# First norm of the last four batches on x loaded with channels on partitions

## Chip, cores and metric

One core of a Trainium2 chip runs the whole program. The metric is the device time of one execution in microseconds (us), smaller is better. "About the same" means within 0.3% of the time before, which is about what a measurement of this kernel can tell from no change.

## The reference

One RWKV block in float32 on x of 8 batches, 256 tokens and 512 channels (32 heads of 16). Cut to what matters here:

```python
def _ln(x, w, b):
    m = jnp.mean(x, axis=-1, keepdims=True)
    v = jnp.mean((x - m) ** 2, axis=-1, keepdims=True)
    return (x - m) * jax.lax.rsqrt(v + EPS) * w + b
...
xn = _ln(x, ln1_w, ln1_b)                      # the first norm
sx = _token_shift(xn, state[:, i1])            # previous token minus this one
xxx = jnp.tanh((xn + sx * maa_x) @ maa_w1)...  # five mixes of xn and sx
w, r, k, v, g = ...                            # decay and four projections
s = k v^T + w * s;  out = r (u * k v^T + s)    # scan over 256 tokens, per head
x = x + groupnorm(out) * g @ Wo.T
xn2 = _ln(x, ln2_w, ln2_b)                     # the second norm
x = x + sigmoid(xr @ ffn_Wr.T) * (square(relu(xk @ ffn_Wk.T)) @ ffn_Wv.T)
```

The sums of a norm run over the 512 channels of one token; `w` and `b` are per channel.

## The kernel before

**Stages.** Each batch b goes through three functions: `inputs_of_scan` (line 677: first norm, mixes, projections of k, v, r, g and the decay w), `scan` (line 829: the recurrence over tokens) and `rest` (line 914: group norm, output projection, second norm, feed-forward). The stages of neighbouring batches overlap: while batch b is in its scan, batch b+1 or b+2 has its inputs made and batch b-1 its rest.

**Layouts.** Projections and the scan want channels on partitions and tokens along a row (tiles `xn`, `sx`, `mix`: 128 channels x 2 x 256 tokens, two of each per batch). x in DRAM has tokens first, so `load_x` (line 510) loads it with tokens on partitions, and `normed` (line 560) makes the norm there: for batches 2 to 7 ScalarE sums x and its squares (lines 571 and 575), takes the root as exp(-0.5 ln) (lines 556 and 558), and line 598 applies factor and shift, which in this layout are one number per partition, into `xh`. Then `turned` (line 603) turns `xh` with eight 128x128 transposes on TensorE per batch and norm (line 614, with the identity `idt`), ScalarE moves them out of PSUM with the channel's `ln_w` and `ln_b` (line 624), writes the first column (the previous row of the state, line 617), and GpSimd subtracts (line 628, tile `sx`).

**The scan.** A batch has 16 pieces of 128 partitions x 4 x 256. SyncE loads each piece of v from DRAM (tile `vs`, six buffers), ScalarE writes its first column (line 882), VectorE multiplies by k (line 889), VectorE scans (line 891), GpSimd multiplies by r (line 894), and after four pieces TensorE sums over the states (line 902).

**TensorE** does nearly all its matmuls through `mul` (line 430), either with all 128 columns of the array, or in four column tiles of 32, whichever the neighbours use. The trace writes them 128\*128 and 128\*32.

**The order of the work.** No scheduler at run time: `Plan` records every operation, and the table `TURNS` gives each its rank. `Plan.order` takes the operations by rank, as their inputs and buffers allow, and lays them into five fixed queues: TensorE, VectorE, ScalarE, GpSimd and SyncE (nearly all DMAs). Each queue runs strictly in its order, so an operation that waits holds back all behind it on that engine. Its tables `LATENCY`, `LANDS` and `TAKES` say how long it thinks that things take.

**Pools that matter.** `xt` (one buffer for the loaded x of batches 2 to 7), `xh` (2), `xn` (4), `x2` (2, x for the rest), `sq` (2, squares in the rest).

Of the kernel before, what the change touches and what calls it, by code (L numbers as in the profile page):

```python
# [12 lines left out]
P = 128  # L13
# [8 lines left out]
EPS = 1e-5  # L22
HALF = 0.5
# [47 lines left out]
class Plan:  # L71
# [5 lines left out]
    LANDS = {"vs__": (2.44, 1.6), "s": (0.1, 1.7), "vo_": (0.4, 1.9), "vo__": (0.46, 1.5), "o_": (0.4, 1.6), "x": (2.3, 1.1), "xt": (1.65, 2.1),  # L77
# [55 lines left out]
    def stage(self):  # L133
# [236 lines left out]
def tile_rwkv_block(  # L370
    ctx: ExitStack,
    tc: tile.TileContext,
    x: bass.AP,
    vecs: bass.AP,
    state: bass.AP,
    consts: bass.AP,
# [747 lines left out]
```

## Time and profile before

| what | value |
|---|---|
| median of 3 runs | 608.28 us (608.18 to 609.9) |
| the profiled execution's own time | 608.87 us |
| its span, first to last instruction | 607.1 us |
| TensorE busy | 597.6 us (98%) |
| VectorE busy | 531.2 us (87%) |
| ScalarE busy | 513.3 us (85%) |
| GpSimd busy | 505.4 us (83%) |
| granted TensorE clock | 1.0 |

In profile rows PE is TensorE, PEld its weight loads, DVE VectorE, ACT ScalarE, POOL GpSimd and SPq the queue of SyncE. "L614" is line 614 of the kernel before; the changed kernel has other numbers. A row of a group ends with busy us, mean ns of one instruction, then the idle time of the engine just ahead of them and what ended it. A row of the timeline begins with the start and the length in us. A float32 matmul is two instructions in the trace, a transpose is one. Ends of matmuls are modelled, so starts are used where a length matters.

### The profile page before, as it was taken

What the parts mean: (1) busy time and instruction counts of PE and PEld (TensorE: products, weight loads), DVE (VectorE), ACT (ScalarE), POOL (GpSimd) and SP (SyncE); (2) the same over time, 40 slices, a digit from 0 to 9 for tenths busy, and PEclk for the clock granted to TensorE, in tenths of its full rate; (3) what the DMA queues carried; (4) which work ended last, traced back from release to release, by engine and by line L of the source; (5) the groups of instructions that cost most, each with busy time, mean ns of one, the idle gap of its engine ahead of it and who ended that gap; (6) DMA issues with size and microseconds to landing.
All of it is one profiled execution on the core that took longest, in us unless ns stands there. A gap on an engine that the chain in (4) does not pass through costs nothing.

```text
span 607.1 us, 18838 instructions
## 1 busy us (share of the span) xinstructions
PE 597.6 (98%) x7892; PEld 344.4 (57%) x7892; DVE 531.2 (87%) x481; ACT 513.3 (85%) x1199; POOL 505.4 (83%) x385
## 2 busy tenths in 40 slices
PE   8999999999999999999999999999999999999997
PEld 7575655467444574377544774465644454745464
DVE  6699999899999989799798999999999999994332
ACT  4898879999999999999999999999998688963431
POOL 1699999999989897899979898989989989887030
PEclk9999999999999999999999999999999999999999
DMA  9796688898778868486589597795876798961551
GB/s 292 251 246 163 143 205 207 223 263 219 205 210 252 231 189 231 138 233 174 164 256 238 143 270 219 225 228 148 271 212 174 204 252 220 265 194 43 177 185 65
DMA packets 52500, 124.85 MB, mean 206 GB/s; under 512 B 5824, under 2 KB 11200, under 8 KB 52416
## 3 DMA queue, kind: packets, MB, share of 16 engines
q1 hardware_dynamic: 48048, 119.46, 71.8%
q10 hardware_dynamic: 4368, 4.20, 2.2%
q8 instruction: 62, 1.02, 0.7%
q14 instruction: 22, 0.18, 0.1%
HBM read 115.25 MB, written 8.39 MB: 204 GB/s over the span
## 4 chain that ended last, share of the span: by engine, by line
PE 88%; ACT 6%; DMA 4%; DVE 2%; issue 1%; SPq 0%; DVEq 0%; ACTq 0%
PE ps L430 73%; PE ps L902 9%; PE ps L614 2%; PE ps L766 2%; DMA Wk<-in_wk 2%; ACT ps L714 1%; DMA mw2a<-in_maa_w 1%; ACT sq L957 1%; DMA x<-in_x 1%; PE ps L928 1%; ACT L1048 1%; PE ps L844 1%; ACT rk L957 1%; ACT mix L984 0%; DVE x L974 0%
## 5 line engine op out<-in xcount | busy, mean ns | idle before, releaser
L891 DVE TENSOR_TENSOR_SCAN st<-wrep,vs 128x1024 f32<-128x1024 f32 x128 | 288.9, 2279 | 4.3 <-ACT wrep L872 2.2
L894 POOL TENSOR_TENSOR st<-st,r 128x1024 f32<-128x1024 f32 x128 | 254.2, 2002 | 11.3 <-DVE st L891 10.4
L889 DVE TENSOR_TENSOR vs<-vs,ps 128x1024 f32<-128x1024 f32 x122 | 144.6, 1208 | 9.3 <-ACT vs L882 6.5
L430 PE MATMUL ps<-Ws,mix 128*32 128x512 f32 (+2 forms) x804 | 114.7, 589 | 0.5 <-DVE x L974 0.2
L430 PEld LDWEIGHTS ps<-Ws,mix 128*32 128x32 f32 (+1 forms) x804 | 38.8, 118 | 62.7 <-issue 55.6
L726 POOL TENSOR_TENSOR mix<-mix,xn 128x512 f32<-128x512 f32 x62 | 67.0, 1096 | 7.7 <-DVE mix L720 6.8
L902 PE MATMUL ps<-st,con 128*32 128x256 f32 x1024 | 62.6, 380 | 0.3 <-DVE x L974 0.2
L430 PE MATMUL ps<-mix,Wg 128*32 128x256 f32 (+1 forms) x784 | 60.2, 379 | 0.3 <-ACT mix L983 0.2
L430 PE MATMUL ps<-mix,Wv 128*32 128x256 f32 (+1 forms) x832 | 59.9, 380 | 0.2 <-DVE mix L723 0.2
L430 PE MATMUL ps<-mix,Wr 128*32 128x256 f32 (+1 forms) x688 | 59.9, 380 | 0.0
L430 PE MATMUL ps<-mix,Wk 128*32 128x256 f32 (+1 forms) x880 | 59.4, 380 | 0.2 <-DMA Wk<-in_wk 0.2
L430 PE MATMUL ps<-mix,Ws 128*32 128x256 f32 (+1 forms) x784 | 58.2, 379 | 0.0
L430 PE MATMUL ps<-Ws,g 128*32 128x512 f32 (+1 forms) x416 | 57.1, 593 | 0.0
L1048 ACT ACT_TABLE_LOAD x39 | 50.0, 1283 | 1.1 <-ACT v L797 0.4
L647 POOL TENSOR_TENSOR mix<-mix,xn 128x512 f32<-128x512 f32 x44 | 47.2, 1093 | 3.1 <-ACT mix L645 2.9
L430 PEld LDWEIGHTS ps<-mix,Wr 128*32 128x32 f32 (+1 forms) x688 | 39.3, 123 | 17.9 <-issue 1.4
L714 ACT ACTIVATE ps<-ps,vec 128x256 f32<-128x256 f32 x112 | 45.7, 445 | 4.2 <-PE ps L430 2.7
L430 PEld LDWEIGHTS ps<-mix,Wv 128*32 128x32 f32 (+1 forms) x832 | 37.9, 116 | 19.5 <-issue 1.1
L902 PEld LDWEIGHTS ps<-st,con 128*32 128x32 f32 x1024 | 34.1, 110 | 26.3 <-issue 5.1
L430 PEld LDWEIGHTS ps<-mix,Ws 128*32 128x32 f32 (+1 forms) x784 | 39.6, 118 | 16.4 <-DVE mix L640 0.6
L430 PEld LDWEIGHTS ps<-mix,Wg 128*32 128x32 f32 (+1 forms) x784 | 38.4, 118 | 18.2 <-issue 1.0
L430 PEld LDWEIGHTS ps<-mix,Wk 128*32 128x32 f32 (+1 forms) x880 | 36.8, 114 | 20.6 <-issue 2.4
(116 smaller groups left out, 935.3 us busy)
## 6 DMA issues: line engine op xcount, KB each, us to landing
vs<-vo SPq DMA_DIRECT2D x128, 512.0 KB, 5.6
Ws<-in_wo SPq DMA_DIRECT2D x16, 512.0 KB, 6.6
Ws<-in_fr SPq DMA_DIRECT2D x16, 512.0 KB, 6.0
Ws<-in_fk SPq DMA_DIRECT2D x16, 512.0 KB, 5.6
Ws<-in_fv SPq DMA_DIRECT2D x16, 512.0 KB, 4.7
x<-in_x SPq DMA_DIRECT2D x9, 512.0 KB, 6.4
vo<-v ACTq DMA_DIRECT2D x15, 256.0 KB, 4.9
out<-o SPq DMA_DIRECT2D x15, 256.0 KB, 4.6
```

Of the source, the lines that this page charges most:

```text
L430: nc.tensor.matmul(out[i : i + n], lhsT=w[:, i : i + n], rhs=x, start=first, stop=final)
L614: nc.tensor.transpose(ps()[:, m, n * P : (n + 1) * P], xh[n]()[:, k * P : (k + 1) * P], idt())
L647: gp(512, t, [t, xn[q]], lambda q=q, t=t: nc.gpsimd.tensor_tensor(t(), t(), xn[q]()[:, :, 1 : T + 1], ALU.add))
L714: act(256, p_, [p_, vec], lambda g=g, q=q, m=m, p_=p_: nc.scalar.activation(p_()[:, m, :], p_()[:, m, :], AF.Identity, bias=col(f"maa_{g}" ...
L726: gp(512, t, [t, xn[q]], lambda q=q, t=t: nc.gpsimd.tensor_tensor(t(), t(), xn[q]()[:, :, 1 : T + 1], ALU.add))
L766: nc.tensor.matmul(pd()[i : i + 32, 0, :], lhsT=w, rhs=src[k // 2]()[:, k % 2, :], start=(k == begin), stop=(k == end))
L889: dve(4 * T, [vs], [vs, kp], lambda m=m, vs=vs, kp=kp: nc.vector.tensor_tensor(vs(), vs(), kp()[:, m : m + 1, :].to_broadcast([P, 4, T]), ...
L891: dve(4 * T, [st], [w, vs], lambda w=w, vs=vs, st=st: nc.vector.tensor_tensor_scan(st().rearrange("p n t -> p (n t)"), w().rearrange("p n ...
L894: gp(4 * T, st, [st, r], lambda m=m, st=st, r=r: nc.gpsimd.tensor_tensor(st(), st(), r()[:, m : m + 1, :].to_broadcast([P, 4, T]), ALU.mul ...
L902: nc.tensor.matmul(pat()[32 * i : 32 * i + 32, 0, :], lhsT=con()[:, s : s + 32], rhs=done[i]()[:, j, :], start=(j == 0), stop=(j == 3),)
L957: act(256, rsb, [rs], lambda blk=2 * q + n, n=n, rows=rows, rsb=rsb: nc.scalar.copy(by_block(rsb)[rows, n, :], rs()[32 * blk : 32 * blk + ...
L1048: nc.scalar.preload_act_table_set(TABLES[table])
```

## The change

For batches 4 to 7 the first norm no longer turns anything on TensorE. x is also given to the program as a second input `xt` with channels on partitions (made when the inputs are laid out, like the other layouts). The new function `ahead`:

- loads x with tokens on partitions, in two halves into `xh`, only for its sums, which are taken in place as before;
- puts factor and minus mean times factor side by side into a small tile `rn` (128 x 2 x 2), with the same ln and exp on ScalarE and the same small product on GpSimd;
- writes `rn` to DRAM (`ms`, 512 numbers of 4 bytes) and reads it back into a tile of the pool `sq` so that every partition holds all 256 factors and 256 shifts (`rb`, 256 KB written);
- loads `xt` into `xn`, multiplies by the factors on VectorE, adds the shifts on GpSimd, then applies `ln1_w` and `ln1_b` on ScalarE in place, and goes on as before.

Pool `xt` is gone, so batches 2 and 3 load x into `x2`; `xn` has six buffers. `LANDS` gets entries for the new loads. `TURNS` is new as a whole: the order changes from the first rows on, in batches 0 to 3 too.

```diff
+AHEAD = (4, 5, 6, 7)
...
     TURNS = """
-        11 45 15 38 49 98 95 96 109 46 94 72 220 97 55 62 64 140 16 14 26 20 27 43 18 54 58 17 40 48 19 60 61,
...
-    pool("xt", 1, [P, NT, E])
...
+    pool("rn", 1, [P, 2, NT])
-    pool("xn", 4, [P, 2, T + 1])
+    pool("xn", 6, [P, 2, T + 1])
...
+    pool("ms", 2, [2, T], dram)
...
     def load_x(b, kind):
-        if b or kind != "xt":
-            t = new("x2" if kind == "xt" and b == 1 else kind, f"{kind}{b}")
+        if kind != "xt" or b and b not in AHEAD:
+            t = new("x2", f"{kind}{b}")
             load(t, x[b].rearrange("(n p) e -> p n e", p=P), 524)
         else:
-            t = [new("sq", f"xt0_{n}") for n in range(NT)]
+            t = [new("xh" if b else "sq", f"xt{b}_{n}") for n in range(NT)]
...
+    def ahead(b):
...
+        act(2, rn, [mv, eh], lambda: nc.scalar.activation(
+            rn()[:, 0, :], mv()[:, :, 1], AF.Ln, bias=eh()[:, 0:1], scale=over), "exp", 1)
+        act(2, rn, [rn], lambda: nc.scalar.activation(rn()[:, 0, :], rn()[:, 0, :], AF.Exp, scale=-0.5), "exp")
+        gp(2, rn, [mn, rn], lambda: nc.gpsimd.tensor_tensor(rn()[:, 1, :], mn(), rn()[:, 0, :], ALU.mult), 30)
+        dma(ms, lambda: rn(), lambda: ms().rearrange("s (n p) -> p s n", p=P), 2, rn)
+        dma(rb, lambda: ms().rearrange("s t -> (s t)").unsqueeze(0).to_broadcast([P, 2 * T]),
+            rb, 262, ms)
...
+        for q in range(NQ):
...
+            dma(xn, lambda q=q: xt[b][:, 2 * q : 2 * q + 2, :], lambda xn=xn: xn()[:, :, 1 : T + 1], 262)
+            dve(512, [xn], [xn, rb], lambda xn=xn: nc.vector.tensor_tensor(
+                xn()[:, :, 1 : T + 1], xn()[:, :, 1 : T + 1], rb()[:, 0:T].unsqueeze(1).to_broadcast([P, 2, T]), ALU.mult))
+            gp(512, xn, [xn, rb], lambda xn=xn: nc.gpsimd.tensor_tensor(
+                xn()[:, :, 1 : T + 1], xn()[:, :, 1 : T + 1], rb()[:, T : 2 * T].unsqueeze(1).to_broadcast([P, 2, T]), ALU.add))
+            for m in range(2):
...
+                act(256, xn, [xn, vec], lambda m=m, k=k, xn=xn: nc.scalar.activation(
+                    xn()[:, m, 1 : T + 1], xn()[:, m, 1 : T + 1], AF.Identity, bias=col("ln1_b", k), scale=col("ln1_w", k)), pointers=2)
...
-        xn, sx = normed(load_x(b, "xt"), 1, 1, b, b == 0)
+        xn, sx = ahead(b) if b in AHEAD else normed(load_x(b, "xt"), 1, 1, b, b == 0)
...
+        "xt": x.reshape(NB, T, NK, P).transpose(0, 3, 2, 1),
```

Two places in the queues. On TensorE, between the projection of r in batch 4 (weights `Wr`) and that of g (`Wg`), the kernel before turns the first norm of batch 5 (`xh` is the norm with tokens on partitions; every row stands once more in the program, which is left out):

```order
L430 MATMUL ps_172<-mix_119,Wr_78 128x256 x2
L614 MATMUL ps_174<-idt,xh_86 128x128
L614 MATMUL ps_174<-idt,xh_87 128x128
...
L614 MATMUL ps_170<-idt,xh_86 128x128
L614 MATMUL ps_170<-idt,xh_87 128x128
...
L430 MATMUL ps_171<-mix_108,Wg_79 128x256 x2
L430 MATMUL ps_171<-mix_109,Wg_80 128x256 x2
```

In the changed kernel the same place on TensorE reads (line 435 is the old 430, 955 the old 902, the sum over states of the scan):

```order
L435 MATMUL ps_174<-mix_118,Wr_77 32x256 x8
L435 MATMUL ps_174<-mix_121,Wr_78 32x256 x8
...
L435 MATMUL ps_178<-mix_116,Wg_79 32x256 x8
L435 MATMUL ps_178<-mix_119,Wg_80 32x256 x8
L955 MATMUL ps_176<-st_161,con 32x256
L955 MATMUL ps_176<-st_156,con 32x256
```

The eight transposes are gone, and the projections around them, which ran with the full array (outputs of 128 partitions), now run in column tiles (32). Counted over the whole queue, TensorE changes between full array, column tiles and row tiles (the mixes and the decay) 82 times before and 72 times now, a transpose counted as full array; the transposes that are gone make no difference to the 82 by themselves.

On VectorE of the changed kernel, in the scan of batch 2, stand the two new products of batch 4 (line 715; 942 is the old 889, 944 the old scan 891, 961 the old 908, 802 the old 749):

```order
L942 TENSOR_TENSOR vs_149<-vs_149,ps_174 128x1024
L1027 TENSOR_TENSOR x_164<-ps_176,x_164 128x512
L961 TENSOR_TENSOR att_140<-ps_175,att_140 128x256
L961 TENSOR_TENSOR att_140<-ps_173,att_140 128x256
L944 SCALAR_TENSOR_TENSOR st_156<-wrep_172,vs_152 128x1024
L715 TENSOR_TENSOR xn_99<-xn_99,sq_163 128x2x256
L802 TENSOR_TENSOR mix_111<-ps_178,sx_107 128x256
L944 SCALAR_TENSOR_TENSOR st_157<-wrep_172,vs_149 128x1024
L715 TENSOR_TENSOR xn_101<-xn_101,sq_163 128x2x256
```

The same stretch of VectorE before (the scan of batch 2) has the scans and products without them:

```order
L974 TENSOR_TENSOR x_161<-ps_172,x_161 128x512
L908 TENSOR_TENSOR att_138<-ps_169,att_138 128x256
L891 SCALAR_TENSOR_TENSOR st_156<-wrep_168,vs_149 128x1024
L974 TENSOR_TENSOR x_161<-ps_173,x_161 128x512
L889 TENSOR_TENSOR vs_146<-vs_146,ps_170 128x1024
L749 TENSOR_TENSOR mix_106<-ps_171,sx_102 128x256
L749 TENSOR_TENSOR mix_108<-ps_169,sx_103 128x256
L891 SCALAR_TENSOR_TENSOR st_152<-wrep_168,vs_146 128x1024
```

Each new product is slipped in behind a scan; the next scan stands behind it.

On SyncE's queue the write of `ms` and the read of `rb` stand among the loads of weights and of `vs`, with four other DMAs between them for the batches 4, 6 and 7 and two for batch 5. Whatever stands behind the read in this queue waits until the write has landed. The queue has 271 DMAs instead of 251. ScalarE's queue has 46 loads of activation tables instead of 40.

More of the change, by code (lines that the diff above doesn't have):

```diff
@@ L76 @@
     LATENCY = {"PE": 0.25, "DVE": 0.13, "ACT": 0.14, "POOL": 0.06, "DMA": 1.65}
-    LANDS = {"vs__": (2.44, 1.6), "s": (0.1, 1.7), "vo_": (0.4, 1.9), "vo__": (0.46, 1.5), "o_": (0.4, 1.6), "x": (2.3, 1.1), "xt": (1.65, 2.1),
+    LANDS = {"vs__": (2.44, 1.6), "s": (0.1, 1.7), "vo_": (0.4, 1.9), "vo__": (0.46, 1.5), "o_": (0.4, 1.6), "ms": (0.4, 2.0), "rb": (0.9, 1.8), "xn__": (0.8, 1.7), "x": (2.3, 1.1), "xt": (1.65, 2.1), "xt_": (0.8, 1.7),
              "Wo_": (1.75, 1.5), "Wfk_": (1.7, 1.5), "Wfr_": (1.75, 1.4), "Wfv_": (1.65, 1.5), "Wg": (1.6, 2.4), "y_": (0.3, 0.6)}
@@ L373, in tile_rwkv_block @@
     x: bass.AP,
+    xt: bass.AP,
     vecs: bass.AP,
@@ L675, in project_tokens @@
         return ps
+    def ahead(b):
+        src = load_x(b, "xt")
+        mv, mn, rn, ms, rb = (new(p, f"{n}{b}") for p, n in (("mv", "mv1_"), ("mn", "mn1_"), ("rn", "rn"), ("ms", "ms"), ("sq", "rb")))
+        if b > 1:
+            for n in range(NT):
+                summed(src[n], mv, [src[n]], lambda n=n: nc.scalar.activation(
+                    src[n](), src[n](), AF.Copy, accum_out=mv()[:, n, 0:1]), 0)
+            act(2, mn, [mv], lambda: nc.scalar.mul(mn(), mv()[:, :, 0], -1.0 / E))
+            for n in range(NT):
+                summed(src[n], mv, [src[n], mn], lambda n=n: nc.scalar.activation(
+                    src[n](), src[n](), AF.Square, bias=mn()[:, n : n + 1], accum_out=mv()[:, n, 1:2]), 1)
+            over = 1.0 / E
+        else:
+            for n in range(NT):
+                st = new("st", f"st1_{b}_{n}")
+                dve(512, [st], [src[n]], lambda n=n, st=st: nc.vector.bn_stats(out=st(), in_=src[n]()))
+                dve(6, [mv], [st], lambda n=n, st=st: nc.vector.bn_aggr(out=mv()[:, n, :], in_=st()), 8)
+            act(2, mn, [mv], lambda: nc.scalar.mul(mn(), mv()[:, :, 0], -1.0))
+            over = 1.0
+        act(2, rn, [mv, eh], lambda: nc.scalar.activation(
[5 more added lines that the diff above has]
+            rb, 262, ms)
+        xns, sxs = [], []
+        i = NVEC + 2 * b + 1
+        for q in range(NQ):
+            xn, sx = new("xn", f"xn1_{b}_{q}"), new("sx", f"sx1_{b}_{q}")
+            dma(xn, lambda q=q: xt[b][:, 2 * q : 2 * q + 2, :], lambda xn=xn: xn()[:, :, 1 : T + 1], 262)
[4 more added lines that the diff above has]
+            for m in range(2):
+                k = 2 * q + m
+                act(256, xn, [xn, vec], lambda m=m, k=k, xn=xn: nc.scalar.activation(
+                    xn()[:, m, 1 : T + 1], xn()[:, m, 1 : T + 1], AF.Identity, bias=col("ln1_b", k), scale=col("ln1_w", k)), pointers=2)
+            act(2, xn, [vec], lambda q=q, xn=xn: nc.scalar.copy(xn()[:, :, 0:1], vec()[:, 2 * q : 2 * q + 2, i : i + 1]))
+            gp(512, sx, [xn], lambda xn=xn, sx=sx: nc.gpsimd.tensor_tensor(
+                sx(), xn()[:, :, 0:T], xn()[:, :, 1 : T + 1], ALU.subtract))
+            xns.append(xn)
+            sxs.append(sx)
+        return xns, sxs
```

240 rows, old and new, of the table TURNS are left out of this document.

## The prediction

> **What bounds the kernel now.** I read the page first, then the busy times by stretch, then who waits for whom.
>
> ```profile
> PE 597.6 (98%) x7892; PEld 344.4 (57%) x7892; DVE 531.2 (87%) x481; ACT 513.3 (85%) x1199; POOL 505.4 (83%) x385
> PE 88%; ACT 6%; DMA 4%; DVE 2%; issue 1%; SPq 0%; DVEq 0%; ACTq 0%
> ```
>
> TensorE is busy 98% of the span and makes up 88% of the chain that ended last. An average can hide a stage with another limit, so the next view splits the span: first filling, the batches 0 to 2, the stretch in which the first norms of the batches 4 to 7 lie, the last scans, and the tail. Columns are length, then busy us of PE, PEld, DVE, ACT, POOL, then granted clock and DMA share.
>
> ```profile
> 0.00:30.00 30.00, 26.63 (x304) 19.93 (x304) 19.10 (x47) 19.75 (x49) 11.97 (x22) 1.00 0.85 273
> 30.00:200.00 170.00, 168.67 (x2528) 98.37 (x2516) 164.69 (x133) 156.34 (x367) 165.79 (x119) 1.00 0.81 209
> 200.00:450.00 250.00, 249.81 (x3299) 143.57 (x3295) 230.57 (x189) 237.67 (x566) 223.86 (x170) 1.00 0.77 213
> 450.00:553.00 103.00, 102.64 (x1536) 55.29 (x1532) 101.34 (x86) 80.08 (x185) 93.46 (x69) 1.00 0.74 202
> 553.00:608.00 55.00, 49.88 (x264) 27.28 (x255) 15.48 (x29) 19.47 (x36) 10.30 (x9) 0.99 0.37 129
> ```
>
> From 200 to 450 us TensorE is idle for 0.19 us out of 250, at full clock. So in that stretch time taken from TensorE's own work comes off the span, as long as the others keep up. They are not far behind: there VectorE is idle for 19.4 us, ScalarE for 12.3, GpSimd for 26.1. And from 450 to 553 VectorE is at 98.4%, with TensorE idle for only 0.36 us.
>
> **What is removed from TensorE.** These are timeline rows at the four places where a first norm of the batches 4 to 7 is turned, each with the row behind it, and ahead of them one turn of a second norm that stands between tiled work:
>
> ```profile
> 203.30 1.08 PE L614 MATMUL ps<-idt,xh 128*128 128x128 f32 x8
> 204.31 1.09 PE L430 MATMUL ps<-w,dw 64*32 64x256 f32 x32
> ...
> 214.10 1.09 PE L614 MATMUL ps<-idt,xh 128*128 128x128 f32 x8
> 215.03 5.34 PE L430 MATMUL ps<-mix,Wg 128*128 128x256 f32 x24
> ...
> 287.31 1.04 PE L614 MATMUL ps<-idt,xh 128*128 128x128 f32 x8
> 288.18 3.62 PE L430 MATMUL ps<-mix,Wg 128*128 128x256 f32 x16
> ...
> 360.38 1.04 PE L614 MATMUL ps<-idt,xh 128*128 128x128 f32 x8
> 361.25 2.97 PE L430 MATMUL ps<-mix,Ws 128*128 128x256 f32 x13
> ...
> 407.81 1.09 PE L614 MATMUL ps<-idt,xh 128*128 128x128 f32 x8
> 408.74 3.60 PE L430 MATMUL ps<-Ws,g 128*128 128x512 f32 x8
> ```
>
> From start to next start the four take 0.93, 0.87, 0.87 and 0.93 us, together 3.6 us. Nothing takes their place on TensorE. The turn at 203.30, between tiled neighbours, took 1.01 until the next start, 0.14 more than one between full-array neighbours; that is two changes of form, so I price one at 0.07 us. The new order has 72 of them instead of 82, which is 10 x 0.07 = 0.7 us less (bounds 0, if other waits cover them, and 1.4, if one change costs the whole 0.14). So TensorE loses 4.3 us of work.
>
> **What is added on VectorE.** Eight products, two for each of the four batches, both inputs in SBUF. The trace has none with a broadcast factor; the nearest rows are products and sums of the same 128x512 size from SBUF. The first two rows are instructions of a line (durations least, median, most), the others timeline rows.
>
> ```profile
> L966 DVE TENSOR_TENSOR g<-att,g x2: 691/692/692, 563.8 to 565.2; 128x512 f32<-128x512 f32 x2
> L723 DVE TENSOR_TENSOR mix<-mix,xn x2: 681/894/1107, 17.6 to 19.6; 128x512 f32<-128x512 f32 x2
> ...
> 19.17 1.03 POOL L628 TENSOR_TENSOR sx<-xn 128x512 f32<-128x512 f32 x1
> 19.65 1.11 DVE L723 TENSOR_TENSOR mix<-mix,xn 128x512 f32<-128x512 f32 x1
> ...
> L894 POOL TENSOR_TENSOR st<-st,r 128x1024 f32<-128x1024 f32 x59 | 117.2, 2004 | 8.3 <-DVE st L891 8.3
> ```
>
> Line 966 ran in the tail and took 0.69. The second product of line 723 met a GpSimd operation that had begun 0.48 us earlier and ended at 20.20; it itself ended at 20.76, 0.56 behind that. It seems to have waited until GpSimd was through. In the steady stretch GpSimd is busy for 223.86 of 250 us, and half of that is line 894 with 2.0 us each. A product that comes at a random moment waits for half of what runs there: up to 1.0 us, 0.55 where it is one of the 1.1 us operations. I take 0.8, nearest to line 894 as the commonest. So one product costs 0.69 + 0.8 = 1.5 us, all eight 11.9 (bounds: 8 x 0.69 = 5.5 if they meet no wait; 8 x 2.7 = 21.6 if each meets a whole line 894). The Trainium skill, "SBUF — State Buffer", section "Who interferes with whom", says that a VectorE instruction with two SBUF inputs and a GpSimd instruction that reads SBUF exclude each other, and whichever issued first keeps the port pair for its whole instruction. The row at 19.65 agrees for one GpSimd operation; no row shows whether a waiting product is let in before the next one. By the row the eight cost 11.9 us, by the rule anything from there to the 28 us of the third rival.
>
> These 11.9 us fall into VectorE's 19.4 us of idle time, but everything is also to end 4.3 us earlier there. What remains is 19.4 - 11.9 - 4.3 = 3.2 us in 246, so VectorE would be 98.7% busy, about as in the stretch 450 to 553. That stretch shows what such a load costs TensorE: 0.36 us of 103, so 0.9 in 246. I put down 0.9 us of new waits on TensorE (bounds 0 and 4.3: behind the latter VectorE ends it, a rival).
>
> **What else is added**, each with its cover.
>
> ```profile
> L726 POOL TENSOR_TENSOR mix<-mix,xn 128x512 f32<-128x512 f32 x25 | 26.9, 1092 | 0.5 <-DVE mix L716 0.4
> L1048 ACT ACT_TABLE_LOAD x39 | 50.0, 1283 | 1.1 <-ACT v L797 0.4
> L598 ACT ACTIVATE xh<-xt,nm,rs x12: 798/814/834, 32.4 to 405.0; 128x512 f32<-128x512 f32 x12
> s<-in_state SPq DMA_DIRECT2D x8, 32.0 KB, 5.3
> vo<-v ACTq DMA_DIRECT2D x15, 256.0 KB, 4.9
> vs<-vo SPq DMA_DIRECT2D x128, 512.0 KB, 5.6
> DMA packets 52500, 124.85 MB, mean 206 GB/s; under 512 B 5824, under 2 KB 11200, under 8 KB 52416
> SPq L419 <- DVE st L891: 263.2, 91, 7.8
> L889 DVE TENSOR_TENSOR vs<-vs,ps 128x1024 f32<-128x1024 f32 x60 | 70.9, 1209 | 6.4 <-ACT vs L882 3.7 <-ACT ps L870 2.6
> L891 DVE TENSOR_TENSOR_SCAN st<-wrep,vs 128x1024 f32<-128x1024 f32 x59 | 133.5, 2280 | 2.4 <-ACT wrep L872 1.3
> ```
>
> GpSimd: eight additions of 1.09 us, 8.7 us, into 26.1 idle. ScalarE: eight times line 598 goes (8 x 0.81 = 6.5 us), six table loads come (6 x 1.28 = 7.7): 1.2 us net into 12.3 idle. Uncovered they would cost that much. The scaling with the channel's factors remains, from SBUF instead of PSUM. SyncE: the write of `ms` and the read of `rb` one behind the other take about 5.3 + 4.9 = 10 us until landed, by the small load of the state and by a transfer of 256 KB; 512 separate numbers may take longer, and the trace has no such write. The read can hold SyncE for up to 5.3 us, and loads of `vs` stand behind it. But SyncE spends 263 us waiting for scans to free a `vs` buffer, and each of the six buffers comes round about every 6 x 4.2 = 25 us (60 products of line 889 in 250 us), of which load (5.6), product (1.2) and scan (2.3) take about 9: cover of some 16 us. So I cost it at nothing; without the cover, up to 5 us for each batch would reach VectorE. The DMAs grow by about 3 MB on 124.85, at a DMA share of 0.77, and TensorE waits for none in that stretch: nothing. `rb` holds one of two `sq` buffers, which the rest's squares want once per batch, and batches 2 and 3 take an `x2` buffer from the rest: nothing as long as the fixed order keeps these apart, else a wait of ScalarE or of a load that has its 12.3 us or its queue's slack to go into.
>
> **The sum.** 608.87 (profiled) - 3.6 - 0.7 + 0.9 = 605.5. The profiled execution lies 0.6 above the median of 608.28, so the forecast is 604.9 us. The new order in the first 200 us, where TensorE is idle 3.37 + 1.33 = 4.7 us, could gain or lose some of that; I sum it at zero, with 1.5 either way in the range, since the waits there are short:
>
> ```profile
> PE ps L614 <- DMA idt<-in_consts: 1.0, 1, 1.0
> PE ps L430 <- DMA Ws<-in_consts: 0.7, 1, 0.7
> ```
>
> **The rivals.** Measured against 608.28, 0.3% is 1.8 us: faster means below 606.5, slower above 610.1; that is what a measurement of this kernel can tell from no change.
>
> *The full gain and a better start.* No product meets a wait that counts, each change of form saves 0.14, and the identity, which now is loaded ahead of the second batch's x, ends the first of the two waits above: 608.28 - 3.6 - 1.4 - 1.0 = 602.3. For it speaks that TensorE hardly waits for VectorE anywhere at 92 to 98% load; against it that VectorE gets work just there. Chance 0.15.
>
> *The gain is given back in waits.* VectorE keeps up only just: of the 11.9 us, a third reaches TensorE through the scans, 4 us, because each queue is fixed and a late product makes the scan behind it late. 608.28 - 4.3 + 4.0 = 608.0. The same time comes out if the new order makes as many new waits in the first batches. Chance 0.18.
>
> *VectorE becomes the bound (slower).* The place is the new products between scans. GpSimd runs nearly without a pause; if a waiting product is not let in at the end of the operation under way but has to wait for the next too, it costs 0.69 + 0.8 + 2.0 = 3.5 us, eight 28 us, which is 8.6 more than VectorE's 19.4 idle: 608.28 + 8.6 = 616.9, and TensorE's gain is worth nothing. It decides from 19.4 / 8 = 2.4 us for one product on; at 2.7, a whole line 894 each time, the time is 608.28 + 2.2 = 610.5. Against the dear end: while VectorE waits it makes no scans, and GpSimd soon has nothing to do, so it must let go. I price the rival at 611. By the rule of the skill's page above, issue order alone decides, which would leave this rival open. Chance 0.13.
>
> *The forecast*, TensorE's gain kept, 603.4 to 606.4 by its bounds: chance 0.54. So faster 0.54 + 0.15 = 0.69, same 0.18, slower 0.13. The range from 601.5 to 609.5 leaves out most of the slower rival and a little of the fast one.
>
> **What would show it.** Right: line 614 down from 128 to 96 transposes, TensorE's busy time down by about 4 us, its idle time between 200 and 440 us below 2 us, and the new products at 0.7 to 2.5 us, mean 1.5. The lock is shown if a product's end follows the end of a GpSimd operation by about 0.56. Wrong: products above 2.4 us in the mean, or TensorE waiting for sums of the scan (line 955 of the new kernel) by more than 3 us in all, or SyncE's queue waiting for the landing of `ms` with ScalarE's first columns of `vs` late behind it. If the time comes out the same with TensorE's work 4 us shorter, the place of the new idle time says which rival it was.

## The result, and the profile after

The changed kernel takes 629.56 us (median of 4 runs, 628.58 to 633.0) against 608.39 for the kernel before on the same chip: a ratio of 1.035, 95% interval 1.031 to 1.040. I had forecast 604.9 us and a range up to 609.5. It is slower by 21 us. The profiled execution took 629.4 us, its span is 627.6.

The page of the changed kernel: TensorE is busy 96% instead of 98%, and DMA has grown from 4% to 10% of the chain that ended last.

```profile
PE 599.8 (96%) x8172; PEld 350.5 (56%) x8172; DVE 536.1 (85%) x489; ACT 513.8 (82%) x1197; POOL 517.3 (82%) x393
PE 68%; DMA 10%; ACT 8%; POOL 5%; DVE 4%; issue 3%; SPq 0%; ACTq 0%; DVEq 0%; POOLq 0%
```

By stretch, with the columns of the table before:

```profile
30.00:200.00 170.00, 164.70 (x2516) 96.57 (x2520) 161.83 (x131) 154.12 (x362) 166.06 (x118) 0.99 0.80 203
200.00:450.00 250.00, 234.96 (x3405) 134.62 (x3398) 216.96 (x184) 213.35 (x517) 213.02 (x161) 0.98 0.77 206
450.00:553.00 103.00, 103.00 (x1468) 60.24 (x1471) 101.02 (x78) 94.05 (x209) 95.55 (x70) 1.00 0.81 222
```

From 200 to 450 us TensorE is now idle for 15.0 us, not 0.2, and VectorE, ScalarE and GpSimd all do less work than before in the same 250 us: no engine has become the bound, all four wait. But idle time is not the whole loss: the granted TensorE clock is 0.98 in this stretch, not 1.00. It was 0.50 in three places, each of which follows a stop of TensorE (of 2.1, 5.5 and 2.9 us; after two other stops, of 2.2 and 3.1 us, it stayed at 1.00):

```profile
198.30:201.70 3.40, 3.40 (x32) 1.35 (x32) 3.28 (x4) 3.33 (x10) 1.81 (x2) 0.50 1.03 282
358.75:365.50 6.75, 5.04 (x64) 2.22 (x68) 5.56 (x5) 6.62 (x14) 5.04 (x4) 0.50 0.97 330
423.60:426.95 3.35, 2.57 (x25) 1.19 (x29) 2.38 (x3) 3.33 (x8) 1.79 (x2) 0.50 1.08 270
```

At half the clock the 11.0 busy us of these rows are worth 5.5 at the full one. The run without the write, below, has the same 8172 matmuls at a clock of 1.0, and there they keep TensorE busy for 593.2 us instead of 599.8. So an estimated 6 of the 21 us are longer matmuls. That the stops bring the low clock is suggested by the order in time, and not shown by itself.

The waits say for what (engine and line that waits, what it waits for, us in total, times, longest):

```profile
ACT vs L935 <- DMA vs<-vo: 22.3, 5, 6.7
DVE vs L942 <- ACT vs L935: 22.9, 8, 6.8
SPq L424 <- DMA ms<-rn: 16.9, 4, 6.7
SPq L424 <- POOL rn L706: 11.3, 3, 7.2
```

ScalarE waits for loads of `vs`, VectorE for ScalarE's first columns. SyncE's queue waits four times, once for each batch, for the landing of `ms`. This is the sign that the prediction gave for its being wrong. The issues by size (KB, median us to landing), and around the write for batch 6 SyncE's timeline:

```profile
ms<-rn SPq DMA_DIRECT2D x4, 2.0 KB, 10.5
sq<-ms SPq DMA_DIRECT2D x4, 256.0 KB, 7.7
```

```profile
342.54 0.37 SPq L424 DMA_DIRECT2D ms<-rn  x1
343.01 1.19 SPq L424 DMA_DIRECT2D vs<-vo  x2
344.25 0.58 SPq L424 DMA_DIRECT2D s<-in_state  x1
349.42 0.35 SPq L424 DMA_DIRECT2D xh<-in_x  x1
354.08 0.33 SPq L424 DMA_DIRECT2D sq<-ms  x1
...
362.17 6.74 SPq L424 DMA_DIRECT2D vs<-vo  x4
```

The write is issued at 342.54, the read at 354.08, and the next loads of `vs` behind it only at 362.17. But this is not all. The two loads of `vs` at 343.01 were issued before the read, so nothing in the queue held them back, and yet they landed late. First the view of `vs` from 342 to 345 us in the changed kernel, then that of the kernel before from 200 to 450 us, and last the store of `vo` that ScalarE's own queue issued at 348.0 in the changed kernel (4.9 us in the median before):

```profile
DMA to landing us min/median/max: 13.8/14.4/15.1
```

```profile
DMA to landing us min/median/max: 4.3/5.3/10.7
```

```profile
L919 ACTq DMA_DIRECT2D vo<-v x1: 366/366/366, 348.0 to 348.0; - x1
DMA to landing us min/median/max: 14.1/14.1/14.1
```

The busy times of the changed kernel show why (last two columns: DMA share and GB/s), and below them the same clock time in the kernel before:

```profile
342.00:348.00 6.00, 6.00 (x116) 3.63 (x112) 5.90 (x6) 5.15 (x14) 6.00 (x8) 1.00 0.07 11
348.00:354.00 6.00, 5.87 (x38) 4.67 (x30) 5.67 (x4) 4.39 (x10) 4.85 (x5) 1.00 0.13 26
354.00:360.00 6.00, 1.01 (x5) 0.55 (x3) 0.66 (x1) 1.18 (x4) 2.14 (x3) 0.89 1.02 301
```

```profile
342.00:348.00 6.00, 6.00 (x65) 4.50 (x67) 5.87 (x6) 5.65 (x11) 5.20 (x4) 1.00 0.47 115
348.00:354.00 6.00, 6.00 (x120) 3.60 (x116) 5.87 (x5) 5.97 (x18) 6.00 (x5) 1.00 1.01 303
```

For the 12 us between this write and its read, the core's DMAs move 11 to 26 GB/s instead of some 200 (the other three writes follow in a table below). Once the write has landed they run at 301, but by then the engines have used up their tiles and stand still for most of 6 us, TensorE included.

### The profile page after: what moved, and what is told of

Its sections match the earlier page's. It is cut to its first block, busy times and chain, and to the rows that moved or that the text cites. A ratio compares the mean times of both kernels' runs of the same rounds, so it can differ in the third digit from the quotient of the medians.

```text
span 627.6 us, 19472 instructions
## 1 busy us (share of the span) xinstructions
PE 599.8 (96%) x8172; PEld 350.5 (56%) x8172; DVE 536.1 (85%) x489; ACT 513.8 (82%) x1197; POOL 517.3 (82%) x393
## 4 chain that ended last, share of the span: by engine, by line
PE 68%; DMA 10%; ACT 8%; POOL 5%; DVE 4%; issue 3%; SPq 0%; ACTq 0%; DVEq 0%; POOLq 0%
PE ps L435 58%; DMA vs<-vo 9%; PE ps L955 7%; POOL st L947 2%; DVE st L944 2%; PE ps L819 1%; PE ps L620 1%; ACT rk L1010 1%; DMA Ws<-in_wv 1%; ACT att L905 1%; ACT L1101 1%; DVE vs L942 1%; POOL mix L653 1%; POOL sx L634 1%; ACT att L1016 1%
## 5 line engine op out<-in xcount | busy, mean ns | idle before, releaser
L947 POOL TENSOR_TENSOR st<-st,r 128x1024 f32<-128x1024 f32 x128 | 255.1, 2008 | 11.9 <-DVE st L944 11.6
L435 PEld LDWEIGHTS ps<-Ws,mix 128*32 128x32 f32 (+1 forms) x828 | 40.4, 117 | 60.4 <-issue 52.6
L435 PE MATMUL ps<-mix,Wk 128*32 128x256 f32 (+1 forms) x928 | 61.8, 388 | 5.2 <-issue 3.1
L435 PE MATMUL ps<-mix,Wr 128*32 128x256 f32 (+1 forms) x784 | 61.3, 389 | 4.0 <-DVE vs L942 3.1
L935 ACT ACTIVATE vs<-s,cm 128x4 f32<-128x4 f32 x128 | 36.0, 296 | 23.2 <-DMA vs<-vo 22.3
L435 PEld LDWEIGHTS ps<-mix,Wk 128*32 128x32 f32 (+1 forms) x928 | 39.7, 115 | 25.0 <-issue 7.3
L435 PEld LDWEIGHTS ps<-mix,Wr 128*32 128x32 f32 (+1 forms) x784 | 40.7, 120 | 21.9 <-issue 4.4
L955 PEld LDWEIGHTS ps<-st,con 128*32 128x32 f32 x1024 | 35.8, 110 | 25.2 <-issue 6.2
L435 PEld LDWEIGHTS ps<-mix,Wg 128*32 128x32 f32 (+1 forms) x808 | 40.8, 117 | 15.4 <-issue 0.9
L905 ACT COPY att<-ps 32x256 f32<-32x256 f32 x128 | 46.5, 363 | 2.5 <-PE ps L897 0.8
```

The lines of the kernel that those rows point to most:

```text
L435: nc.tensor.matmul(out[i : i + n], lhsT=w[:, i : i + n], rhs=x, start=first, stop=final)
L905: act(350, atts[q], [pc], lambda i=32 * (2 * q + m), m=m, q=q, h=32 * h: nc.scalar.copy(atts[q]()[h : h + 32, m, :], pc()[i : i + 32, 0, :]))
L935: act(4, vs, [s0, cm], lambda i=i, blk=blk, vs=vs: nc.scalar.activation(vs()[:, :, 0:1], s0()[:, blk, 4 * i : 4 * i + 4].rearrange("p (n o ...
L947: gp(4 * T, st, [st, r], lambda m=m, st=st, r=r: nc.gpsimd.tensor_tensor(st(), st(), r()[:, m : m + 1, :].to_broadcast([P, 4, T]), ALU.mul ...
L955: nc.tensor.matmul(pat()[32 * i : 32 * i + 32, 0, :], lhsT=con()[:, s : s + 32], rhs=done[i]()[:, j, :], start=(j == 0), stop=(j == 3),)
```

## Two theories, and the runs that tell them apart

*Queue theory*: the read of `rb` waits in SyncE's queue until the write has landed, and loads of `vs` stand behind it. *Stall theory*: the write of 512 separate numbers itself stops the other transfers. Beside them stood the lock rival of the prediction (VectorE's new products) and the new order as such. Times are medians; a ratio is to runs of the kernel before that go with it on the same chip (609.04, 608.62, 609.02, 609.06 and 608.82 us), with its 95% interval.

**The write stays, the read no longer waits for it.**

```diff
-        dma(rb, lambda: ms().rearrange("s t -> (s t)").unsqueeze(0).to_broadcast([P, 2 * T]),
+        dma(rb, lambda: x[b, 0:1, :].to_broadcast([P, 2 * T]),
             rb, 262, ms)
```

> The write of the 512 numbers stays, but the read of rb takes its bytes from a row of x, so it no longer waits until the write has landed (the norms of the batches 4 to 7 come out with other numbers). Queue theory (SyncE's queue is held by the waiting read, 7 to 12 us for each batch, and loads of vs stand behind it): the hold is gone, so the time falls to 605 to 611 us. Stall theory (while the 512 pieces of 4 bytes are under way nearly no other transfer moves, 11 GB/s at 342 to 348 us against 207 before, so loads issued behind land in 14 to 15 us instead of 6): the write is still there, the time stays at 621 to 630 and loads of vs issued right behind a write still land after more than 10 us. Lock theory (VectorE's new products) and order theory (the new table of turns itself is slow): 628 to 630.

625.58 us, ratio 1.027 (1.025 to 1.029). The stall theory holds: with the wait of the read gone only 4 to 5 of the 21 us are gone. The loads of `vs` right behind the write at 341.87 still land late, though they were issued at once (elsewhere SyncE's queue still waits for a landing of `ms`, 4.2 us in all instead of 16.9):

```profile
DMA to landing us min/median/max: 12.9/13.6/14.3
```

**Neither write nor wait.** The line that writes `ms` is kept in the plan but issues nothing; `rb` is read from x as above.

> Neither the write of ms nor the wait for it: rb is read from a row of x, all else, the order of the queues included, is as in the changed kernel (the norms of the batches 4 to 7 come out with other numbers). Queue theory and stall theory: both expect 603 to 608 us, near my forecast of 604.9, TensorE's idle time at 200 to 450 us down from 15 to about 2. Lock theory and order theory: 626 to 630, since products, sums and order are all there.

608.98 us, ratio 1.0001 (0.9987 to 1.0015). So write and wait together cost the 21 us; order, products, sums and loads together cost no more than TensorE gains. But 608.98 is not the forecast of 604.9 either. TensorE idles 3.1 us of this stretch:

```profile
200.00:450.00 250.00, 246.89 (x3622) 136.96 (x3624) 237.30 (x195) 230.46 (x550) 234.37 (x176) 1.00 0.81 220
```

**Neither write nor wait nor products.** As the last, and the eight products are left out.

> As the run without the write of ms (609.0 us where I had forecast 604.9 without any cost of the detour), and the eight new products on VectorE are left out as well (the norms of the batches 4 to 7 come out with other numbers). There the products took 1.1 us in the median and up to 2.2, and TensorE's idle time at 200 to 425 us was 3.5 us longer than in the kernel before, by the count of its starts. Theory that VectorE's load gives the gain of the transposes back: without the products the time falls by 3 to 5 us, to 604 to 606. Theory that the new order (its first batches, the places at 200, 330 and 407 us) gives it back: 608 to 609.5.

606.29 us, ratio 0.996 (0.994 to 0.997); the profiled execution, the fastest of five, took 604.42 us. The idle time in the stretch is gone:

```profile
200.00:450.00 250.00, 249.68 (x3706) 135.71 (x3709) 233.73 (x193) 234.29 (x560) 235.06 (x178) 1.00 0.83 225
```

So the products give back 2.7 us of what TensorE gains (by the two intervals, an estimated 1.3 either way).

**The products left out, write and wait kept.**

> The eight new products on VectorE are left out (xn is not multiplied by the factor), all else stays, write and wait too. Lock theory: VectorE loses 5.6 to 12 us of work at the place where it was short, the time falls to 610 to 620 us. Queue, stall and order theory: 627 to 630.

622.3 us, ratio 1.021 (1.019 to 1.023). Neither side had it right: 7 us go by the medians and 8.6 by the ratios, more than the others allowed, and what remains lies above the 610 to 620 of the lock rival. In the changed kernel the products take only 6.5 us in all, with hardly a wait ahead of them:

```profile
L715 DVE TENSOR_TENSOR xn<-xn,sq 128x512 f32<-128x512 f32 x8 | 6.5, 835 | 0.7 <-DMA sq<-ms 0.6
```

Part of it is the granted clock: 0.994 to 0.997 in the four executions of this run, 0.985 to 0.995 in those of the changed kernel, which by the means is an estimated 0.006 x 620 = 3.7 us. That VectorE, which has scans to catch up with after each stall, passes on each us of work would explain the rest; no run shows it by itself.

**The write alone, in the kernel before.**

```diff
+            loads += op.engine == "DMA" and op.bufs[0].name.startswith("vs")
+            if op.engine == "DMA" and op.bufs[0].name.startswith("vs") and loads in (45, 64, 79, 92):
+                nc.sync.dma_start(out=ms.rearrange("s (n p) -> p s n", p=P), in_=vec()[:, 0, 0:4].rearrange("p (s n) -> p s n", s=2))
```

> The kernel before, with four extra writes of 512 numbers of 4 bytes to DRAM, each issued on SyncE's queue right behind a load of vs at about 183, 267, 338 and 392 us; nobody reads them and nothing waits for them. Stall theory: each stops nearly all transfers for about 10 us, and a good part of this comes through as late loads of vs: 10 to 18 us more than before, 619 to 627 us, with the DMA share near 0.1 for some us behind each write. Queue theory (only a read that waits for the landing costs): 608 to 610.

624.31 us, ratio 1.026 (1.022 to 1.031). Four writes of 2 KB that nobody reads cost 15.7 us, nearly 4 us each. The profiled execution, at a granted clock of 1.0 throughout, took 622.1, so most of this needs no low clock. The writes land after the same 10.5 us, and ScalarE waits 15.5 us for `vs`, against 0.5 in the kernel before:

```profile
ms<-vec SPq DMA_DIRECT2D x4, 2.0 KB, 10.5
ACT vs L882 <- DMA vs<-vo: 15.5, 8, 5.4
```

**The same four writes in pieces of 16 bytes** instead of 4, the bytes the same.

```diff
-                nc.sync.dma_start(out=ms.rearrange("s (n p) -> p s n", p=P), in_=vec()[:, 0, 0:4].rearrange("p (s n) -> p s n", s=2))
+                nc.sync.dma_start(out=ms.rearrange("s t -> (s t)").rearrange("(p j) -> p j", p=P), in_=vec()[:, 0, 0:4])
```

> The kernel before with the same four extra writes, but each as 128 pieces of 16 bytes instead of 512 of 4 (with 512 of 4: 10.5 us to landing and 624.3 us in all, 15.7 more than before). If the stall goes with the number of pieces: landing in about 3.6 us as in the run with wide writes, a quarter of the cost, 610 to 614 us. If any write of a few bytes stops the other transfers for as long, whatever its pieces: 10 us and 620 to 627. If the 16 bytes are long enough for no stall: 608 to 610, and the 7 us by which the run with wide writes was slower than the one without a write came from the strided product and sum.

609.7 us, ratio 1.0011 (0.9996 to 1.0025): no cost that can be measured. It is the cutting into 512 pieces of 4 bytes, not the write as such. Number and size of the pieces change together here, and with them which partitions write neighbouring numbers in DRAM, so which of these it is stays open. The landing was not the 3.6 us that I expected:

```profile
ms<-vec SPq DMA_DIRECT2D x4, 2.0 KB, 5.4
```

**Pieces of 16 bytes in the changed kernel**, three ways: with a strided product and sum, so that all is computed as it should be; with plain reading, so that the numbers come in another order; and plain without the wait.

```diff
-        dma(ms, lambda: rn(), lambda: ms().rearrange("s (n p) -> p s n", p=P), 2, rn)
+        dma(ms, lambda: rn().rearrange("p s n -> p (s n)"), lambda: ms().rearrange("s t -> (s t)").rearrange("(p j) -> p j", p=P), 2, rn)
```

> The same numbers are written as 128 pieces of 16 bytes instead of 512 of 4, and the product and the sum pick them out of rb with a stride; the read still waits for the landing. If the time of the write goes with the number of pieces, it lands in about 10.5 / 4 = 2.6 us and at least 2 us of fixed time more, some 5 us. Queue theory: the hold is about half as long, 608 to 618 us. Stall theory: the stall is a quarter as long, 605 to 612. If the landing stays at 10 us, both say 629. Lock theory and order theory: 628 to 632, the strided products being no shorter.

> As the run with wide writes (616.1 us, 7.1 more than without a write), but product and sum read rb without a stride, so that factors and shifts come in another order of the tokens and the norms of the batches 4 to 7 are others. Four extra wide writes alone cost the kernel before 0.7 us. If the 7 us come from the read that waits for the write's landing (SyncE's queue held): 613 to 616 us. If they come from the strided reading (products 1.52 us in the mean instead of 1.21, sums 1.67 instead of 1.24): 608 to 611.

> As the run before it in this call, and rb is read from a row of x, so that nothing waits for the write. Stall theory, as it stands after the run with extra wide writes (pieces of 16 bytes stop nothing): 608 to 611 us, as without a write, where the same kernel with 512 pieces of 4 bytes took 625.6. If SyncE's queue is held by the write itself, which has to wait for GpSimd's rn (11.3 us in all in the changed kernel): 612 to 616.

Strided 616.05 us, ratio 1.011 (1.007 to 1.014); plain 608.46, ratio 0.9990 (0.9977 to 1.0004); plain without the wait 608.11, ratio 0.9986 (0.9972 to 1.0000). With pieces of 4 bytes out of the way, the read that waits costs nothing that can be measured: the write lands in 3.8 us here. Nor does it cost anything measurable that SyncE's queue waits for GpSimd's `rn` before three of the four writes, 11.3 us in all in the changed kernel and in the last of these three runs. The run with strides, which alone would have left a doubt, was slow for the strides: its products and sums took 1.52 and 1.67 us in the mean, those of the plain run 1.21 and 1.23.

```profile
L717 POOL TENSOR_TENSOR xn<-xn,sq 128x512 f32<-128x512 f32 x8 | 13.2, 1668 | 1.3 <-DVE xn L715 1.3
L715 DVE TENSOR_TENSOR xn<-xn,sq 128x512 f32<-128x512 f32 x8 | 12.0, 1520 | 0.0
```

```profile
L717 POOL TENSOR_TENSOR xn<-xn,sq 128x512 f32<-128x512 f32 x8 | 9.8, 1234 | 1.3 <-DVE xn L715 1.3
L715 DVE TENSOR_TENSOR xn<-xn,sq 128x512 f32<-128x512 f32 x8 | 9.6, 1215 | 0.0
```

**Pieces of 8 bytes, all computed.** Partition p gets the tokens 2p and 2p + 1, so the two factors of a partition are neighbours in `ms`.

```diff
-                dma(t[n], lambda n=n: x[b, n * P : (n + 1) * P, :], t[n], 262)
+                dma(t[n], lambda n=n: x[b, n:T:NT, :] if b else x[b, n * P : (n + 1) * P, :], t[n], 262)
...
-        dma(ms, lambda: rn(), lambda: ms().rearrange("s (n p) -> p s n", p=P), 2, rn)
+        dma(ms, lambda: rn(), lambda: ms().rearrange("s (p n) -> p s n", p=P), 2, rn)
```

> The changed kernel's order and all its work, with one change: the halves of x that are loaded for the sums hold the even and the odd tokens instead of the first and the last 128, so that the two factors of a partition belong to neighbouring tokens and are written as one piece of 8 bytes: 256 pieces of 8 bytes instead of 512 of 4, and product and sum read rb without a stride. If only pieces of 4 bytes stop the other transfers (none at 16 bytes): 608 to 610 us, landing in about 4 us, as the run with wide writes and plain reading (608.5). If pieces of 8 bytes stop them too, half as many: landing in 5 to 6 us, 614 to 620.

610.46 us, ratio 1.0019 (1.0003 to 1.0036). Two lines take back 19 of the 21 us. A small cost of the pieces of 8 bytes is not excluded: the run with plain pieces of 16 had 0.9990 (0.9977 to 1.0004). The write lands in 5.0 us, and SyncE's queue waits for it only once, 2.0 us:

```profile
ms<-rn SPq DMA_DIRECT2D x4, 2.0 KB, 5.0
SPq L424 <- DMA ms<-rn: 2.0, 1, 2.0
```

How long the other transfers are stalled is seen when the same stretch is taken behind each of the four writes, the 6 us that begin 5 us after its issue:

| kernel | pieces of a write | GB/s behind the four writes |
|---|---|---|
| changed kernel | 512 of 4 bytes | 58, 34, 25, 27 |
| kernel before with four writes | 512 of 4 bytes | 103, 87, 38, 31 |
| changed kernel, pairs | 256 of 8 bytes | 205, 232, 287, 171 |
| changed kernel, wide and plain | 128 of 16 bytes | 226, 189, 256, 184 |
| kernel before with four wide writes | 128 of 16 bytes | 288, 253, 117, 231 |

Wider pieces do not do away with the stall, they shorten it. Nearer to the write the pairs show it too, 64 GB/s from 264 to 269 us behind the write at 263.04, and so does the wide and plain run, 95 GB/s from 264 to 267 behind that at 262.77. The engines hardly notice: ScalarE waits for loads of `vs` for 3.1 us in all with the pairs and 1.7 with the wide and plain pieces, against 2.6 without a write and 22.3 in the changed kernel.

**Tries to beat both.** The same with the products and sums at other places in the order:

> As the run before it in this call, and the eight new products and sums (and the four operations of the last second norm on VectorE) are put at other places in the table of turns, mostly a place or two away, chosen with the landing set to 3.2 and 3.4 us and with a product that waits for GpSimd. Without products the time is 2.7 us below that of the run without a write; a third to a half of this may be had by better places: 606.5 to 609 us, TensorE's idle time at 200 to 450 us below 2 us instead of 3.1. If the pieces of 8 bytes stop other transfers: as above, 613 or more.

610.56 us, ratio 1.0019 (1.0005 to 1.0033): nothing gained. Then three kernels with a table of turns made wholly anew: `rn` turned on VectorE and written in rows; that and the factor copied to PSUM; and no DRAM trip, with four turns of a broadcast column on TensorE for each batch.

```diff
+        dve(32, [row], [rn], lambda: nc.vector.transpose(row()[:, 0:32], rn()[:, 0:32]))
...
+        act(256, pf, [rb], lambda: nc.scalar.copy(pf()[:, 0, :], rb()[:, 0:T]))
...
+                    nc.tensor.transpose(ps()[:, j, n * P : (n + 1) * P], rn()[:, j, n : n + 1].to_broadcast([P, P]), idt())
```

> Meant to beat both: VectorE turns factor and shift in blocks of 32 x 32 (one instruction for a batch), four writes of 4 pieces of 128 bytes bring them to DRAM in the order in which rb reads them, and the table of turns is made anew with a landing of 2.4 us for each write and of 3.4 us for rb. The product still reads two tiles in SBUF. Stall theory: no stall worth mention, TensorE's gain of 4.3 us stays, less what the products give back (2.7 us by the two runs without a write, less where the new order has room for them): 604 to 608 us. If a write of short pieces stalls the other transfers whatever its size: 612 or more.

> As the run before it in this call, and ScalarE copies the 256 factors of a batch from rb into PSUM (one copy of 128 x 256 each), from where the product reads them; turns made anew for this. Lock theory (a product with both inputs in SBUF waits for GpSimd): the products take 0.65 to 0.75 us each, none over 1 us, instead of 0.69 to 2.2, and the time is 603 to 607 us. If the waits were not the lock, products of over 1 us stay.

> No DRAM trip at all: TensorE turns each of the four columns of factor and shift, read as a broadcast of 128 equal columns, into a 128 x 128 block of PSUM (four turns for a batch instead of eight before, 0.44 us less each by the rows of line 614), the product reads the factor there, ScalarE copies the shift to SBUF for GpSimd's sum; turns made anew. Both theories: no stall and no wait for a landing; of TensorE's gain 4 x 0.44 = 1.7 us remain and up to 0.7 from fewer changes of form, the products cost no lock: 605 to 608 us.

614.87 us, ratio 1.008 (1.005 to 1.011); 615.47, ratio 1.009 (1.006 to 1.012); 610.59, ratio 1.002 (1.000 to 1.004). All miss what I expected; their orders brought new waits (ScalarE for loads of `vs` 7.3, 10.1 and 5.2 us in all), and what of this is the order and what the new work is not settled. The first one's 614.87 lies where I had put a stall by any short write, but SyncE's queue waits only 0.7 us in all for its writes there, and the writes in pieces of 16 bytes speak against it. No version that computes everything beat the kernel before. The second one shows the lock, though. First the eight products with both inputs in SBUF, from the run without a write, then the eight with the factor in PSUM, each of which met a GpSimd operation under way (least, median, most ns):

```profile
L715 DVE TENSOR_TENSOR xn<-xn,sq x8: 685/1135/2151, 198.7 to 408.6; 128x512 f32<-128x512 f32 x8
```

```profile
L733 DVE TENSOR_TENSOR xn<-xn,ps x8: 662/679/690, 204.3 to 411.3; 128x512 f32<-128x512 f32 x8
```

## Why the prediction was wrong, point by point

Put together by ratio, taken in this order: without write, wait and products 0.996; the products add 0.0045 (2.7 us), the write 0.027 (16.6 us), the wait for it 0.008 (4 to 5 us). The shares depend on the order: with the write there, the products were worth 7 to 9 us.

**TensorE's gain: the mechanism right, the size not shown in full.** Line 620, the old 614, has 96 transposes. Without products and write TensorE is busy 591.8 us instead of 597.6. I had the time 4.3 us shorter; by the ratio of that run it is 2.7 shorter (1.7 to 3.7 by the interval). Only its fastest execution, 604.42, comes to what my sum less its 0.9 of new waits gives, 608.87 - 3.6 - 0.7 = 604.6. In the changed kernel itself TensorE's busy time did not fall by 4 us as I wrote, it rose by 2.2, to 599.8, at the lower clock.

**The products: the mechanism right, the size in the sum wrong.** In the run without a write they take 1.21 us in the mean, in the range I gave around 1.5. Of the eight, two met no GpSimd operation under way and took 0.69 us; six met one and ended 0.55 us behind it. Five of these clearly waited for no second operation (the sixth began within 0.03 us of a change from one GpSimd operation to the next), so the question that the lock rival left open is answered for these five: the waiting product was let in before the next. The lock works the other way too, which I did not price: the GpSimd operation behind took 2.45 us instead of 2.00. One of the products, between the two:

```profile
201.51 1.99 POOL L947 TENSOR_TENSOR st<-st,r 128x1024 f32<-128x1024 f32 x1
201.91 2.15 DVE L715 TENSOR_TENSOR xn<-xn,sq 128x512 f32<-128x512 f32 x1
203.47 2.45 POOL L947 TENSOR_TENSOR st<-st,r 128x1024 f32<-128x1024 f32 x1
```

But what this costs TensorE I set at 0.9 us, from the stretch 450 to 553; it is 2.7. So even with a harmless write the rival "the gain is given back in waits", 608.0, would have come true (608.98 without a write), not the forecast.

**SyncE: the step that failed.** "So I cost it at nothing" was wrong three times over. First the price: I took 5.3 us for the landing from a load of 32 KB and wrote that 512 separate numbers may take longer; it was 10.5. With the cover gone I had allowed up to 5 us for each batch; the wait came to 4 to 5 us in all. Second, and worth most, the kind of cost. I looked for who is held *behind* the read in the queue and found cover for that. The write also holds up transfers that do not wait for it in any queue: the loads of `vs` already issued, and the store of `vo` from ScalarE's own queue at 348.0, which took 14.1 us instead of 4.9. That is 16.6 of the 21 us, and no view of the kernel before could show it, since it has no write in such pieces. The range should have been open on that side. The sign that I gave for being wrong came true, but it names the wait in the queue, which is the smaller part; that it pointed to the right place is partly luck. Third, the cover: 16 us is what is left of a buffer's turn of 25 us if its load is issued the moment the buffer is free. Matching, in the trace of the kernel before, 72 loads in their order, from the middle of batch 2 to the end of batch 6, with ScalarE's first columns gives 5.9 us in the median between landing and use, 2.3 or less for one in ten, and 0.4 at the least. The two loads behind the write for batch 6 came 8.5 and 9.8 us later than the median of before (13.8 and 15.1 instead of 5.3). The 263 us that SyncE waits for scans were a sign that loads come just in time, not that there is slack.

**The rival of the lock, 611,** ended on the right side for the wrong reason: in the changed kernel the products meet GpSimd less (0.84 us in the mean), since it too stands still.

**The rest.** ScalarE is busy 513.8 us (513.3 before; I had 1.2 more), GpSimd 11.9 us more (I had 8.7; the sums take 1.34 us each, not 1.09). In the first 200 us TensorE idles 6.0 us in the run without write and products, 4.7 before: within the 1.5 that I allowed for the new order. The forecast's "603.4 to 606.4 by its bounds" holds these 1.5 us alone; with the bounds that I gave for changes of form and new waits it would have been 601.8 to 610.5.

## What to carry to other kernels

Before a small transfer is put into a kernel that lives on its DMAs, count its pieces: a write of 512 pieces of 4 bytes cost nearly 4 us here each time, though only 2 KB move; laying the data out so that neighbours in DRAM come from one partition took nearly all of it back. A transfer is to be costed by what it does to the others in flight, not only by who waits for it in the queue. And cover is measured from landing to use, piece by piece; that a queue waits much for free buffers does not show that there is any. When engines stand still, read the granted clock too.

## What the runs showed of the hardware that was not expected

- A write of 512 numbers of 4 bytes each to DRAM lands in 10.5 us in two different kernels, and in the 6 us that begin 5 us after its issue the core's DMAs move 25 to 58 GB/s in the one and 31 to 103 in the other. 256 pieces of 8 bytes land in 5.0 us, 128 of 16 bytes in 3.6 to 3.8 in the changed kernel and in 5.4 in the kernel before, and the same 6 us then carry 117 to 288. The Trainium skill, "DMA: Bandwidth & Descriptors", section "Specifications", names 512 B as the least for line rate, and a read-modify-write below; the landing times agree in direction, but pieces of 16 bytes, far below that, cost no time that can be measured here. Its section "Back-pressure in remote DMA" says, of transfers between cores, that stalled writes also stall the other queues of the DMA engine that makes them; the store of `vo` (14.1 us from another queue) fits this for a write to DRAM. Which mechanism it is, no run here shows.
- An input read with a stride of 16 bytes from SBUF made products 0.31 us and sums 0.43 us longer, and the time 7 us longer. The Trainium skill, "SBUF — State Buffer", section "Door 1: The DMA port swizzle (why `[64,N]` ≈ `[32,N]`)", says in a note that accesses which cross to a new line of 16 bytes each time pay a penalty; the longer products and sums agree. It gives no size for the penalty.
- Eight products of 128 x 512 on VectorE with one input in PSUM took 0.66 to 0.69 us, though each met a GpSimd operation; with both inputs in SBUF those that met one ended 0.55 us behind it, and the GpSimd operation behind such a product took about 0.45 us longer (2.45 instead of 2.00).
- The granted TensorE clock was 0.50 for 3.4 to 6.8 us in three places of the changed kernel, each behind a stop of TensorE of 2.1 to 5.5 us.
